# Latent attention and ternary gated MLP on one core: the normed attention input transposed by VectorE blocks and through DRAM instead of on TensorE

## The chip, the cores and the metric

The kernel runs on one core of a Trainium2 chip. The metric is the device time of one execution in microseconds (us); lower is better. Three runs of the kernel before took 1197.63 to 1201.61 us, median 1198.27 us.

## The reference, cut to what matters

```python
x = x + layernorm(attn(layernorm(x)))      # x: 4096 rows (2 x 2048) of 512
x = x + layernorm(ffn(layernorm(x)))
# attn(h), per head of 32 (16 heads, 64 latent keys):
Q = h @ Wq.T + bq;  V = h @ Wv.T + bv
logits = Q . latent / sqrt(32)             # top 4 of 64, softmax over these
out = (weights @ latent + V) @ Wo.T + bo
# ffn(h): weights rounded to -1, 0, 1 times a scale
hidden = silu(h @ Wu.T) * (h @ Wg.T)       # 2048 wide
out = hidden @ Wd.T
```

`h @ Wq.T` on TensorE needs h with its 512 features on the partitions: h^T. How h^T of the attention is made is what the change touches.

## The kernel before, in words

The 4096 rows are worked in eight blocks of 512 rows, each four tiles of 128 rows (t = 0 to 3). All instructions stand in an order written by hand, engine by engine; no scheduler moves them, and each engine works its list in order.

The outer loop (L835) goes over the blocks b; for each it runs the expert layer in 16 chunks e of 128 hidden columns. A chunk is, on TensorE: `up("u", e)` (eight 512-column matmuls into `pu`, L602), `up("g", e)` (eight into `pg`, L602), `down(e-1)` (eight into the four accumulators `acc`, L638). On the other engines: `tanh` of `pu` on ScalarE (L611), `silu` (L614) and `gate` (L619) on VectorE, a cast `hi` on ScalarE (L623), the remainder `lo` on VectorE (L628); `down` needs both `hi` and `lo`. `pu` and `pg` have one buffer each, so `up("u", e+1)` waits for `silu(e)`.

Between these chunk steps, at the places `do(3)`, `do(0)`, `do(1)`, `do(2)`, the program puts in the pieces of the attention of block b + 1. The table is in `pieces` (L764): `put(e, k, f, ...)` puts f at chunk e, place k. The first two blocks' attention is written out apart (`FirstAttention`). For block b + 1 >= 2 (six blocks) the start is:

- at chunk 14 place 2 and chunk 15 place 1 of block b - 1: `a_stats` (mean and variance of each row, VectorE, L234 and L235) and `a_rstd` (POOL, L241 and L242);
- at chunk 0 of block b: `a_apply` (VectorE, L261) writes the normed rows of a tile into a `row` buffer; `a_trans` (L299) makes 4 TensorE transposes of 128 by 128 per tile into PSUM (`pt_a`, L271), 16 per block, and ScalarE copies them into `hT` (L307);
- at chunk 1 place 0: `q(0)` (L310, matmuls at L314), the first reader of `hT`; at places 1 of chunk 1 `l(0)` (logits, L328); further `q`, `l`, `v` (L406) later.

At chunk 0 and 1 the previous block is also finished: `down(15)` runs in chunk 0, then `y_stats` (VectorE), `y_rstd` (POOL), and in chunk 1, behind `gate(1)`, four `y` (VectorE, L261) read the accumulators, which `down(0)` of the new block then overwrites.

One step of the kernel before already transposes by VectorE and DRAM: `z` (L381). VectorE transposes the weights `w` in blocks of 32 by 32 (L383), SP writes the tile `z` to DRAM (`dz`, L388), and four loads of 64 KB each fetch it back with the 32-row groups exchanged (`wT`, L391). All DMAs of the kernel are issued by SP's queue, in program order, and a DMA whose data isn't ready holds up all behind it.

The tiles of x: `load_x(b + 2)` at chunk 4 of block b (chunk 12 for b = 0), into twelve buffers (3 * TT). The same tile feeds the norm, and later the residual sums.

Of the kernel before, what the change touches and what calls it, by code (L numbers as in the profile page):

```python
# [10 lines left out]
F32 = mybir.dt.float32  # L11
F32R = mybir.dt.float32r
BF16 = mybir.dt.bfloat16
AF = mybir.ActivationFunctionType
# [3 lines left out]
P = 128  # L18
# [40 lines left out]
def latent_attention_ternary_glu(  # L59
# [15 lines left out]
    nc = tc.nc  # L75
    NT, D = x_in.shape
    E = wuT.shape[1]
    DC = D // P
    EC = E // P
    TB = 512  # L80
    TT = TB // P
    NB = NT // TB
# [4 lines left out]
    work = ctx.enter_context(tc.tile_pool(name="work", bufs=2))  # L87
    small = ctx.enter_context(tc.tile_pool(name="small", bufs=4))
    dram = ctx.enter_context(tc.tile_pool(name="dram", bufs=3, space=bass.MemoryType.DRAM))
# [7 lines left out]
    def at_psum(name):  # L97
        return ps_at.tile([P, 512], F32, tag="at", name=name)
# [7 lines left out]
    def transposed(which, b, name, dtype):  # L106
        return work.tile([P, DC, TB], dtype, tag=f"{which}{b % 2}", name=name, bufs=1)


    x_tiles = {}  # L110
# [6 lines left out]
    raw = {}  # L117
    late = []
    for q in range(DC):
        w = work.tile([P, D], F32, tag="x", name=f"raw_d_6_{q}", bufs=3 * TT)  # L120
        late.append(w)
    for n, i in RAW_ORDER:
        raw[n, i] = wpool.tile([P, CH], F32, tag="chunk", name=f"raw_{n}_{i}", bufs=6 * DC)
# [4 lines left out]
    def load_x(b):  # L128
        x_tiles[b] = []
        for t in range(TT):  # L130
            xt = work.tile([P, D], F32, tag="x", name=f"x_{b}_{t}", bufs=3 * TT)
            r = b * TB + t * P
            nc.sync.dma_start(out=xt, in_=x_in[r : r + P, :])
            x_tiles[b].append(xt)

    def load_up(n, src):
        for i, (k, h) in enumerate(halves):
            nc.sync.dma_start(
                out=raw[n, i], in_=src[k * P : (k + 1) * P, h * CH : (h + 1) * CH]
            )  # L140
# [5 lines left out]
    bqv_sb = wpool.tile([P, 2, DC], F32, name="bqv_sb")  # L146
# [13 lines left out]
    for i in range(count["d"]):  # L160
        rows = 2 * P if i < 6 else P
        r = i * 2 * P if i < 6 else 12 * P + (i - 6) * P
        nc.sync.dma_start(
            out=raw["d", i].rearrange("p (c n) -> p c n", n=D),
            in_=wdT[r : r + rows, :].rearrange("(c p) n -> p c n", p=P),
# [99 lines left out]
    def row(name):  # L265
        return work.tile([P, D], F32, tag="row", name=name, bufs=4)

    def transpose_row(h, name):
        pt = at_psum(f"pt_{name}")
        for c in range(DC):  # L270
            nc.tensor.transpose(pt[:, c * P : (c + 1) * P], h[:, c * P : (c + 1) * P], ident)  # L271
        return pt.rearrange("p (c k) -> p c k", k=P)
# [3 lines left out]
    class Attention:  # L276
# [9 lines left out]
            self.po = {}  # L286


        def a_stats(self, t):
            self.norm_a.stats(t, x_tiles[self.b][t])  # L290

        def a_rstd(self, lo, hi):
            self.norm_a.rstd(lo, hi)

        def a_apply(self, t):
            self.rows["a", t] = row(f"h_a{self.b}_{t}")
            self.norm_a.apply(self.rows["a", t], x_tiles[self.b][t], t)

        def a_trans(self, t, engine=None):  # L299
            if self.hT is None:  # L300
                self.hT = transposed("X", self.b, f"hT_{self.b}", F32)
            src = transpose_row(self.rows.pop(("a", t)), f"a{self.b}_{t}")
            dst = self.hT[:, :, t * P : (t + 1) * P]
            if engine is nc.vector:
                nc.vector.tensor_copy(dst, src)
            else:
                nc.scalar.copy(dst, src)  # L307


        def q(self, c):  # L310
# [65 lines left out]
            )  # L376

        def z(self, i):  # L381
            z = work.tile([P, 4, P], F32, tag="left", name=f"z_{self.b}_{i}", bufs=2)
            nc.vector.transpose(  # L383
# [11 lines left out]

        def mixed(self, x):
            return x.rearrange("p (t a i) -> p a t i", t=TT, i=32)

# [9 lines left out]

        def y(self, c):
            self.y_pe(c)
            nc.scalar.activation(
                self.mixed(self.attnT[:, c, :]),
                self.pv.pop(c).rearrange("p (a t i) -> p a t i", t=TT, i=32),
                AF.Identity, bias=bqv_sb[:, 1, c : c + 1],
            )

        def y_pe(self, c):
            for pr in range(2):  # L420
# [53 lines left out]


    class FirstAttention(Attention):
        def a_trans_pe(self, t):
            if self.hT is None:
                self.hT = transposed("X", self.b, f"hT_{self.b}", F32)
            self.pt = getattr(self, "pt", {})  # L480
            self.pt[t] = transpose_row(self.rows.pop(("a", t)), f"a{self.b}_{t}")
# [178 lines left out]
    A = FirstAttention(0)  # L660
# [81 lines left out]
    for step in FIRST_STEPS.split():  # L742
        name, numbers = re.fullmatch(r"([a-z]+)([0-9_]*)", step).groups()
# [20 lines left out]
    def pieces(A, after):  # L764

        at = {(e, k): [] for e in range(EC) for k in range(4)}

        def put(e, k, f, *args):
            at[e, k].append(lambda: f(*args))

        if A.b > 1:
            put(0, 0, A.a_apply, 0)
            put(0, 0, A.a_apply, 1)
            put(0, 1, A.a_trans, 0)
            put(0, 1, A.a_trans, 1)
            put(0, 1, A.a_apply, 2)
            put(0, 1, A.a_apply, 3)
            put(0, 2, A.a_trans, 2)
            put(0, 2, A.a_trans, 3)
            put(1, 0, A.q, 0)  # L780
            put(2, 0, A.q, 1)
            put(4, 0, A.q, 2)
            put(6, 0, A.q, 3)
        put(1, 1, A.l, 0)
        put(2, 2, A.l, 1)
        put(5, 1, A.l, 2)
        put(7, 1, A.l, 3)
        for i in range(8):
            put(2 + i, 0, A.m, i)
            put(2 + i, 2, A.r, i)  # L790
            put(3 + i, 3, A.e, i)
            put(3 + i, 1, A.n, i)
            put(3 + i, 1, A.z, i)
        for c in range(DC):
            put(5 + 2 * c, 1, A.v, c)
            put(5 + 2 * c, 1, A.y, c)
        put(11, 2, A.o, 0)
        put(11, 2, A.o, 1)
        put(11, 2, A.o_bias, 0)
        put(12, 0, A.o, 2)  # L800
        put(12, 0, A.o_bias, 1)
        put(12, 0, A.o_rstd, 0, 2)
        put(12, 1, A.o, 3)
        put(12, 1, A.o_bias, 2)
        put(12, 2, A.o_apply, 0)
        put(12, 2, A.o_apply, 1)
        put(12, 2, A.o_bias, 3)
        put(12, 2, A.o_rstd, 2, 4)
        put(13, 0, A.o_apply, 2)
        put(13, 0, A.o_apply, 3)  # L810
        put(13, 1, A.f_stats, 0)
        put(13, 1, A.f_stats, 1)
        put(13, 1, A.f_rstd, 0, 2)
        put(13, 2, A.f_stats, 2)
        put(13, 2, A.f_stats, 3)
        put(13, 2, A.f_rstd, 2, 4)
        put(14, 0, A.f_apply, 0)
        put(14, 0, A.f_apply, 1)
        put(14, 1, A.f_alloc)
        put(14, 1, A.f_trans, 0)  # L820
        put(14, 1, A.f_trans, 1)
        put(14, 1, A.f_apply, 2)
        put(14, 1, A.f_apply, 3)
        put(15, 0, A.f_trans, 2)
        put(15, 0, A.f_trans, 3)
        if after is not None:
            put(14, 2, after.a_stats, 0)
            put(14, 2, after.a_stats, 1)
            put(15, 1, after.a_stats, 2)
            put(15, 1, after.a_stats, 3)  # L830
            put(15, 1, after.a_rstd, 0, 4)
        return at

    prev = None
    for b in range(NB):  # L835
        if b > 0:
            A, nxt = nxt, after
        after = None
        F = Experts(b, (A.hi, A.lo))
        at = {}  # L840
        for e in range(EC):
            if e == (12 if b == 0 else 4) and b + 2 < NB:
                load_x(b + 2)
            if e == 4:
                after = Attention(b + 2) if b + 2 < NB else None
                if b + 1 < NB:
                    later = pieces(nxt, after)
                    at.update({k: v for k, v in later.items() if k[0] >= 4})
            elif e == 0 and b + 1 < NB:
                at.update({k: v for k, v in pieces(nxt, None).items() if k[0] < 4})  # L850

            def do(k):
                for f in at.get((e, k), ()):
                    f()

            def first(place):
                if b == 0:
                    rest(e, place)

            F.up("u", e)  # L860
            do(3)
            F.tanh(e)
            first("tanh")
            do(0)
            F.silu(e)
            F.up("g", e)
            do(1)
            F.gate(e)
            F.high(e)
            first("high")  # L870
            if e > 0:
                F.down(e - 1)
            elif prev is not None:
                prev.down(EC - 1)
            do(2)
            if e == 0 and prev is not None:
                for t in range(TT):
                    prev.y_stats(t)
                prev.y_rstd(0, TT)
            if e == 1 and prev is not None:  # L880
                for t in range(TT):
                    prev.y_out(t)
            F.low(e)
        prev = F
# [52 lines left out]
```

## Time and profile before

| | |
|---|---|
| median of three runs | 1198.27 us |
| the profiled execution | 1200.29 us |
| its span, first to last instruction | 1198.5 us |
| mean granted TensorE clock | 0.994 |
| TensorE (PE) busy | 1165.4 us |
| VectorE (DVE) busy | 823.9 us |
| ScalarE (ACT) busy | 376.7 us |
| GpSimd (POOL) busy | 176.6 us |
| share of the end chain on PE | 91% |

The profile is of one execution. Its chain is followed back from the last instruction: each step to what released it, or to the instruction before it on the same engine. In a timeline a row gives the start, the duration, the engine, the line and the operation; `x8` says that eight instructions were merged into the row. A DVE duration is longer than the distance to the next start, since instructions overlap at their ends; where instructions follow each other at once, the distance is what one costs. SPq rows are the times in which SP issues DMAs, not the transfers.

### The profile page before, as it was taken

To read this page: it belongs to the slowest core of one execution; us is meant where nothing else is said; L and a number is where in the kernel's file an instruction comes from. 1 tells how busy PE (TensorE), PEld (TensorE's weight loads), DVE (VectorE), ACT (ScalarE), POOL (GpSimd) and SP (SyncE) were. 2 spreads that over 40 slices of the span, in tenths; PEclk is the share of its full clock that TensorE was granted. 3 is DMA by queue.
4 is the path that set the end of the run, shared out by engine and by line. 5 is a ranking of instruction groups with operands and counts; after the bars stand their busy time and mean duration, and the time that the engine had idled before them with its cause. 6 is when DMAs were issued, how large, how long until landed. Compare 5 with 4: busy or idle time off the path is not lost.

```text
span 1198.5 us, 14533 instructions
## 1 busy us (share of the span) xinstructions
PE 1165.4 (97%) x4814; PEld 791.9 (66%) x4814; DVE 823.9 (69%) x2887; ACT 376.7 (31%) x667; POOL 176.6 (15%) x215
## 2 busy tenths in 40 slices
PE   8999999999999999999999999999999999999996
PEld 5447665765767666666657666676665866657884
DVE  5876984777757766678757687476884868747344
ACT  4884541332213322133222332123321332212221
POOL 1066001210022000320003200032000320013002
PEclk9899999999999999999999999999999999999998
DMA  9700211021100211002110021100210011100000
GB/s 351 272 0 1 70 63 45 1 97 53 62 1 10 97 53 53 1 36 80 53 45 1 36 88 53 36 1 36 97 58 23 1 50 57 56 16 10 27 1 35
DMA packets 56283, 63.61 MB, mean 53 GB/s; under 512 B 6160, under 2 KB 34832, under 8 KB 56208
## 3 DMA queue, kind: packets, MB, share of 16 engines
q1 hardware_dynamic: 56208, 62.68, 15.1%
q8 instruction: 38, 0.62, 0.2%
q14 instruction: 37, 0.30, 0.1%
HBM read 39.59 MB, written 23.07 MB: 52 GB/s over the span
## 4 chain that ended last, share of the span: by engine, by line
PE 91%; DVE 4%; ACT 2%; DMA 1%; POOL 1%; issue 0%; SPq 0%; POOLq 0%; DVEq 0%; ACTq 0%
PE acc L638 20%; PE pu L602 19%; PE pg L602 19%; PE pv L406 8%; PE po L432 8%; PE pq L314 7%; PE pv L421 3%; PE pl L328 2%; PE pq L490 1%; PE pt_f L271 1%; PE pt_a L271 1%; PE po L558 1%; ACT w L336 1%; DMA raw_u<-in_wuT 1%; DMA lk<-in_latk 1%; DVE left L354 1%
## 5 line engine op out<-in xcount | busy, mean ns | idle before, releaser
L638 PE MATMUL acc<-tern_d,hi 128*128 128x512 f32 x512 | 209.7, 410 | 4.1 <-DVE y L261 4.1
L602 PE MATMUL pg<-hT_f,tern_g 128*128 128x512 f32 x512 | 212.7, 415 | 0.8 <-DVE h L619 0.8
L602 PE MATMUL pu<-hT_f,tern_u 128*128 128x512 f32 x512 | 203.8, 398 | 0.7 <-ACT hT_f L579 0.7
L638 PE MATMUL acc<-tern_d,lo 128*128 128x512 f32 x512 | 200.3, 391 | 0.1
L602 PE MATMUL pu<-lT_f,tern_u 128*128 128x512 f32 x512 | 199.5, 390 | 0.2 <-DVE lT_f L585 0.2
L602 PE MATMUL pg<-lT_f,tern_g 128*128 128x512 f32 x512 | 199.5, 390 | 0.0
L623 ACT CAST hi<-h 128x512 fp32r<-128x512 f32 x128 | 79.2, 618 | 255.0 <-DVE h L619 255.0
L611 ACT ACTIVATE h<-pu,columns 128x512 f32<-128x512 f32 x128 | 87.5, 684 | 223.6 <-PE pu L602 223.1
L614 DVE SCALAR_TENSOR_TENSOR h<-h,pu 128x512 f32<-128x512 f32 x128 | 86.9, 679 | 98.2 <-ACT h L611 98.2
L638 PEld LDWEIGHTS acc<-tern_d,hi 128*128 128x128 f32 x512 | 96.1, 188 | 56.4 <-issue 24.4
L619 DVE TENSOR_TENSOR h<-h,pg 128x512 f32<-128x512 f32 x128 | 85.6, 669 | 63.9 <-PE pg L602 63.0
L628 DVE TENSOR_TENSOR lo<-h,hi 128x512 fp32r<-128x512 f32 x128 | 90.3, 706 | 49.0 <-ACT hi L623 49.0
L602 PEld LDWEIGHTS pg<-hT_f,tern_g 128*128 128x128 f32 x512 | 96.2, 188 | 27.5 <-issue 7.4
L602 PEld LDWEIGHTS pg<-lT_f,tern_g 128*128 128x128 f32 x512 | 96.2, 188 | 26.1 <-issue 7.4
L406 PE MATMUL pv<-hT,wv 128*128 128x512 f32 x224 | 102.1, 598 | 10.1 <-ACT w L336 10.1
L602 PEld LDWEIGHTS pu<-hT_f,tern_u 128*128 128x128 f32 x512 | 96.1, 188 | 23.3 <-issue 1.7
L602 PEld LDWEIGHTS pu<-lT_f,tern_u 128*128 128x128 f32 x512 | 96.2, 188 | 21.6 <-issue 1.7
L638 PEld LDWEIGHTS acc<-tern_d,lo 128*128 128x128 f32 x512 | 96.3, 188 | 20.2 <-issue 1.7
L241 POOL TENSOR_SCALAR rs_o<-mv_o 128x2 f32<-128x2 f32 (+1 forms) x18 | 6.4, 355 | 667.9 <-DVE mv_o L235 667.7
L354 DVE MATCH_REPLACE8 left<-m,w 128x64 f32<-128x64 f32 x512 | 100.2, 210 | 0.0
L432 PE MATMUL po<-wo,attnT 128*128 128x512 f32 x224 | 99.5, 592 | 0.0
L439 DVE TENSOR_TENSOR o<-po,bo_sb 128x512 f32<-128x512 f32 x28 | 19.4, 692 | 100.5 <-PE po L432 100.5
(116 smaller groups left out, 1434.2 us busy)
## 6 DMA issues: line engine op xcount, KB each, us to landing
dz<-z SPq DMA_DIRECT2D x56, 256.0 KB, 2.0
wT<-dz SPq DMA_DIRECT2D x224, 64.0 KB, 1.9
x<-in_x SPq DMA_DIRECT2D x32, 256.0 KB, 3.7
out_x<-x SPq DMA_DIRECT2D x32, 256.0 KB, 2.0
raw_u<-in_wuT SPq DMA_DIRECT2D x8, 512.0 KB, 8.4
raw_g<-in_wgT SPq DMA_DIRECT2D x8, 512.0 KB, 10.2
raw_d<-in_wdT SPq DMA_DIRECT2D x6, 512.0 KB, 11.6
wq<-in_wqT SPq DMA_DIRECT2D x1, 1024.0 KB, 8.0
```

Source lines behind the costliest of these rows:

```text
L314: nc.tensor.matmul(pq, lhsT=wq[:, k, c * P : (c + 1) * P], rhs=self.hT[:, k, :], start=(k == 0), stop=(k == DC - 1),)
L354: nc.vector.match_replace(left[:, g, :], m8[:, g, :], w[:, g, :], TAKEN)
L406: nc.tensor.matmul(self.pv[c], lhsT=wv[:, k, c * P : (c + 1) * P], rhs=self.mixed(self.hT[:, k, :]), start=(k == 0), stop=False,)
L421: nc.tensor.matmul(self.pv[c][pr * HP : (pr + 1) * HP, :], lhsT=lv[:, 2 * c + pr, :], rhs=self.wT.pop(2 * c + pr), start=False, stop=True, ...
L432: nc.tensor.matmul(self.po[t], lhsT=self.attnT[:, c, t * P : (t + 1) * P], rhs=wo[:, c, :], start=(c == 0), stop=(c == DC - 1),)
L602: nc.tensor.matmul(p, lhsT=tern[n, 2 * k + e // 8][:, (e % 8) * P : (e % 8 + 1) * P], rhs=part[:, k, :], start=(k == 0 and i == 0), stop=( ...
L611: nc.scalar.activation(self.h[e], self.pu[e], AF.Tanh, scale=half_u[0])
L614: nc.vector.scalar_tensor_tensor(self.h[e], self.h[e], 1.0, self.pu.pop(e), ALU.add, ALU.mult)
L619: nc.vector.tensor_tensor(self.h[e], self.h[e], self.pg.pop(e), ALU.mult)
L623: nc.scalar.copy(hi, self.h[e])
L628: nc.vector.tensor_tensor(lo, self.h.pop(e), self.hid[e][0].bitcast(F32), ALU.subtract)
L638: nc.tensor.matmul(self.acc[t], lhsT=part[:, t * P : (t + 1) * P], rhs=wd, start=(e == 0 and i == 0), stop=(e == EC - 1 and i == 1),)
```

## The change

For the six blocks b >= 2 the TensorE transposes and ScalarE copies are replaced. The rows of x are loaded a second time into four buffers of their own (`xa`); the norm is applied in place there, one chunk place earlier (chunk 15, place 2, of the block before); VectorE transposes each column group of 128 in blocks of 32 by 32 (`a_blocks`, 16 instructions per block); SP writes four tiles `za` to DRAM (`da`) in runs of 512 bytes and issues sixteen loads of 64 KB, which exchange the 32-row groups (`a_load`). The tokens of `hT` then stand in another order, which the transpose of `z` turns back, so the strided reading in `v` stays and the strided write of `attnT` falls away. The place of `q(0)` is not changed.

```diff
-            xt = work.tile([P, D], F32, tag="x", name=f"x_{b}_{t}", bufs=3 * TT)
+            xt = work.tile([P, D], F32, tag="x", name=f"x_{b}_{t}", bufs=2 * TT)
...
+    def load_normed(b):
+        for t in range(TT):
+            xt = work.tile([P, D], F32, tag="xa", name=f"xa_{b}_{t}", bufs=TT)
+            r = b * TB + t * P
+            nc.sync.dma_start(out=xt, in_=x_in[r : r + P, :])
+            normed[b, t] = xt
...
         def a_apply(self, t):
-            self.rows["a", t] = row(f"h_a{self.b}_{t}")
-            self.norm_a.apply(self.rows["a", t], x_tiles[self.b][t], t)
-        def a_trans(self, t, engine=None):
...
+            self.norm_a.apply(normed[self.b, t], normed[self.b, t], t)
+        def a_blocks(self, c):
+            if c == 0:
+                self.da = dram.tile([P, 4, DC, P], F32, tag="da", name=f"da_{self.b}", bufs=2)
+            z = row(f"za_{self.b}_{c}").rearrange("p (k e) -> p k e", k=4)
+            for t in range(TT):
+                nc.vector.transpose(
+                    z[:, :, 32 * t : 32 * t + 32],
+                    normed[self.b, t][:, c * P : (c + 1) * P].rearrange("p (k j) -> p k j", j=32),
+                )
+            nc.sync.dma_start(out=self.da[:, :, c, :], in_=z)
+        def a_load(self):
+            self.hT = transposed("X", self.b, f"hT_{self.b}", F32)
+            for k in range(4):
+                for c in range(DC):
+                    nc.sync.dma_start(
+                        out=self.hT[32 * k : 32 * k + 32, c, :].rearrange("j (a e) -> j a e", a=4),
+                        in_=self.da.rearrange("(a j) k c e -> k c j a e", j=32)[k, c],
+                    )
...
-            put(0, 0, A.a_apply, 0)
-            put(0, 0, A.a_apply, 1)
-            put(0, 1, A.a_trans, 0)
-            put(0, 1, A.a_trans, 1)
-            put(0, 1, A.a_apply, 2)
-            put(0, 1, A.a_apply, 3)
-            put(0, 2, A.a_trans, 2)
-            put(0, 2, A.a_trans, 3)
+            put(0, 0, A.a_blocks, 0)
+            put(0, 0, A.a_blocks, 1)
+            put(0, 1, A.a_blocks, 2)
+            put(0, 1, A.a_blocks, 3)
+            put(0, 1, A.a_load)
             put(1, 0, A.q, 0)
...
             put(15, 1, after.a_rstd, 0, 4)
+            for t in range(TT):
+                put(15, 2, after.a_apply, t)
...
-            if e == (12 if b == 0 else 4) and b + 2 < NB:
-                load_x(b + 2)
+            if e == 4 and 0 < b < NB - 1:
+                load_x(b + 1)
+            if e == (12 if b == 0 else 6) and b + 2 < NB:
+                load_normed(b + 2)
```

More of the change, by code (lines that the diff above doesn't have):

```diff
@@ L119, in latent_attention_ternary_glu @@
     for q in range(DC):
-        w = work.tile([P, D], F32, tag="x", name=f"raw_d_6_{q}", bufs=3 * TT)
+        w = work.tile([P, D], F32, tag="xa", name=f"raw_d_6_{q}", bufs=TT)
         late.append(w)
@@ L134, in load_x @@
             x_tiles[b].append(xt)
+    normed = {}
+    def load_normed(b):
[4 more added lines that the diff above has]
+            normed[b, t] = xt
     def load_up(n, src):
@@ L289, in a_stats @@
         def a_stats(self, t):
-            self.norm_a.stats(t, x_tiles[self.b][t])
+            self.norm_a.stats(t, normed[self.b, t])
         def a_rstd(self, lo, hi):
@@ L295, in a_apply @@
         def a_apply(self, t):
-            self.rows["a", t] = row(f"h_a{self.b}_{t}")
-            self.norm_a.apply(self.rows["a", t], x_tiles[self.b][t], t)
-        def a_trans(self, t, engine=None):
[L300 to L307, printed above, removed]
+            self.norm_a.apply(normed[self.b, t], normed[self.b, t], t)
[17 more added lines that the diff above has]
+                    )
         def q(self, c):
@@ L394, in z @@
                 )
+        mixes = False
         def mixed(self, x):
@@ L412, in y @@
             self.y_pe(c)
[L413 to L417, printed above, removed]
+            dst, src = self.attnT[:, c, :], self.pv.pop(c)
+            if self.mixes:
+                dst, src = self.mixed(dst), src.rearrange("p (a t i) -> p a t i", t=TT, i=32)
+            nc.scalar.activation(dst, src, AF.Identity, bias=bqv_sb[:, 1, c : c + 1])
         def y_pe(self, c):
@@ L476, in latent_attention_ternary_glu, with a_stats, a_apply @@
     class FirstAttention(Attention):
+        mixes = True
+        def a_stats(self, t):
+            self.norm_a.stats(t, x_tiles[self.b][t])
+        def a_apply(self, t):
+            self.rows["a", t] = row(f"h_a{self.b}_{t}")
+            self.norm_a.apply(self.rows["a", t], x_tiles[self.b][t], t)
         def a_trans_pe(self, t):
```

## The prediction

> **What bounds the kernel now.** I read the busy shares first, then the chain that ended last, then the chain in order of time around one block's start.
>
> ```profile
> PE   1165.4 (97%) x4814; PEld 791.9 (66%) x4814; DVE 823.9 (69%) x2887; ACT 376.7 (31%) x667; POOL 176.6 (15%) x215
> ...
> PE 91%; DVE 4%; ACT 2%; DMA 1%; POOL 1%; issue 0%; SPq 0%; POOLq 0%; DVEq 0%; ACTq 0%
> ```
>
> TensorE is busy 97% of the span, and 91% of the chain is its own queue. So a PE instruction taken out is worth its time, and a wait put in front of a PE instruction costs its whole length. The chain at the start of one of the six blocks (the other five look alike):
>
> ```profile
> 515.18 1.81 PE pu L602 x8
> 516.99 1.82 PE pg L602 x8
> 518.81 0.88 PE pt_a L271 x8
> 519.69 1.85 PE acc L638 x8
> 521.54 0.87 PE pt_a L271 x8
> 522.41 1.83 PE pu L602 x8
> 524.24 3.43 PE pq L314 x8
> 527.68 1.84 PE pg L602 x8
> ```
>
> Chunk 0 begins at 515.18. The sixteen transposes lie directly on the chain, in two groups of eight. The first reader of `hT`, q(0), starts at 524.24 with no gap before it: today everything that makes `hT` is hidden but the 1.75 us of the transposes.
>
> **What the change removes.** Per block 0.88 + 0.87 = 1.75 us of PE, six blocks, 10.5 us. Without it PE would be ready for q(0) at 524.24 - 1.75 = 522.49. The ScalarE copies that go (24 of 590 ns) lie on an engine busy 31%; I cost them at nothing. So do the contiguous write of `attnT`: today's strided one takes 688 ns, the contiguous form of the first block 682.
>
> **What it adds: the new way to hT.** I walk it in this block's times. VectorE and POOL before:
>
> ```profile
> 515.53 0.65 DVE L619 TENSOR_TENSOR h<-h,pg 128x512 f32<-128x512 f32 x1
> 516.88 0.69 DVE L628 TENSOR_TENSOR lo<-h,hi 128x512 fp32r<-128x512 f32 x1 [0.69 <-ACT hi L623]
> 517.48 1.00 DVE L261 TENSOR_SCALAR h_a<-x,mv_a,rs_a 128x512 f32<-128x512 f32 x2
> 518.40 0.68 DVE L614 SCALAR_TENSOR_TENSOR h<-h,pu 128x512 f32<-128x512 f32 x1
> ...
> 515.98 1.01 POOL L242 TENSOR_TENSOR rs_a<-rs_a,minus_half 128x4 f32<-128x4 f32 x1
> ```
>
> 1. The four `a_apply` now stand before lo(15). They need rs_a, ready at 515.98 + 1.01 = 516.99. They start near 517.05 and cost 0.46 each (two from 517.48 to 518.40): 4 x 0.46 = 1.84, until 518.89.
> 2. lo(15) takes 0.60 (516.88 to 517.48), until 519.49. Its reader down(15) reaches PE at 518.81 now, so PE stands some 0.6 us; this disappears in the later wait.
> 3. Eight block transposes (c = 0, 1). The trace has no 128x128 one, only the 128x512 of `z`: 711 ns, next start 0.64 later. On VectorE the 512-element tensor_tensor costs 0.60 start to start, the 32-element one 0.10 (L356, L358), that is 0.50 for 480 elements, about 1.04 ns each; 0.64 - 384 x 0.00104 = 0.24 us. Bounds: a quarter of 0.64, 0.16, and the whole 0.64. I take 0.24, as the 128-element form lies nearest to those short ones. 8 x 0.24 = 1.92, until 521.41. silu(0), queued behind them, is done 0.60 later, at 522.01 instead of 519.0; up("u", 1) waits for it, again inside the later wait.
> 4. Eight more (c = 2, 3): until 523.93, the last one's end near 524.0. gate(0), y_stats and lo(0) follow, some 5 us; all are needed only behind q(0).
> 5. SP issues the last `da` write at about 524.05 and its loads behind it. The nearest rows are `dz` and `wT`:
>
> ```profile
> 549.83 0.33 SPq L388 DMA_DIRECT2D dz<-z  x1
> 551.89 1.75 SPq L391 DMA_DIRECT2D wT<-dz  x4
> ...
> wT<-dz SPq DMA_DIRECT2D x224, 64.0 KB, 1.9
> ```
>
> A 256 KB write is followed by its reader 551.89 - 549.83 = 2.06 us after its issue. `da` has the same bytes in 512-byte runs instead of 2 KB; I add 0.2 (bounds 2.06 and 3.9, the longest landing of these rows). So it has landed at 524.05 + 2.26 = 526.3. The loads are issued at 1.75 / 4 = 0.44 us each and land 1.9 after their issue (1.8 to 3.9). Their order is k outer, c inner: the fourth (k = 0, c = 3) is the first that needs the last write, and in the built program the first matmul of q(0) waits for the four loads of c = 0, the last of which is the thirteenth. That is nine steps after the fourth: 526.3 + 9 x 0.44 = 530.26, landed at **532.2**. The other three matmuls of q(0) wait for loads 14, 15, 16, 0.44 apart, and take 0.86 each, so nothing more is lost.
>
> q(0) starts at 532.2 instead of 524.24: **8.0 us later per block**, the 1.75 us of gain already inside. Nothing gives it back: behind q(0) the chain is the same (pg, then gate(1), the first `y`, down(0)), since gate(1) waits for pg(1).
>
> 6. The clock. PE then stands from about 524 to 532. The trace shows one long stand, at the end; the last matmul starts at 1186.36:
>
> ```profile
> 1188.00:1190.00 2.00, 0.00 (x0) 0.00 (x0) 1.97 (x4) 0.00 (x0) 1.72 (x5) 1.00 0.00 0
> 1190.00:1192.00 2.00, 0.00 (x0) 0.00 (x0) 1.61 (x4) 0.00 (x0) 1.82 (x5) 0.67 0.00 0
> 1192.00:1194.00 2.00, 0.00 (x0) 0.00 (x0) 1.63 (x2) 0.00 (x0) 2.00 (x2) 0.50 0.02 6
> ```
>
> Column 7 (after the five engines' busy times) is the granted clock: full until 4 us after the last matmul, then 0.50. And at the start of the program the warm-up matmuls `ones` take 421 ns in the first five us (first start 1.0) and 275 from about 6.1 on. So an 8 us stand should end at half clock, and q(0) and what follows run so for some 3.4 to 5.1 us; half of it is lost. I take 2.2 us, bounds 0 (rival B) and 2.6.
>
> The Trainium skill ("TensorE: Matmul & The Clock Gate", "What's actually happening") says that the clock falls to half after an idle window of about 3.4 us and is given back after one busy window of that length. By it alone the loss would be half of 3.4, 1.7 us, and the time 3 us less; the start of this trace shows a longer slow stretch.
>
> **The other edits.** The second load of x adds four 256 KB DMAs per block at chunk 6, between the issues of two `z` steps; SP issues them in 1.85 us, in a stretch where it otherwise waits for `z`, and `wT` is needed a chunk later (today PE waits for `wT` 0.8 us in all). Nothing; if that cover went, at most 1.85 us per block. The load of x for the residual is needed at chunk 12. The four `da` writes and sixteen loads stand ahead of the `out_x` stores, which wait for POOL until after q(0) anyway. `a_apply` in place of four `row` buffers frees these for `za`.
>
> **The sum.** 8.0 + 2.2 = 10.2 us per block, times six: 61 us. Against the profiled execution: span 1198.5 + 61 = 1259.5, and 1.8 lie around the span (1200.29 - 1198.5): 1261. The profiled execution lies 2.0 above the median of the runs, so for the median 1198.27 + 61 = **1259 us**.
>
> Both ends: low, transposes at 0.16 (16 x 0.08 = -1.3), the write at 2.06 (-0.2), loads issued at the 0.33 of `dz` (9 x 0.11 = -1.0), clock 1.7 (-0.5): 7.2 per block, 1241. High, write (+1.6) and loads (+2.0) landing at 3.9, clock 2.6 (+0.4): 14.2 per block, 1283.
>
> A rule that speaks against the change: the Trainium skill ("VectorE: DVE Perf Modes", "Rules for kernel authors") gives a 128x128 transpose to TensorE where PSUM is a fit destination, and "The three transpose paths" gives 311 ns to VectorE's and 390 to TensorE's. This trace has TensorE's at 0.87 / 8 = 0.11 us, less than the page; with 311 ns for VectorE's an estimate would be 16 x 0.07 = 1.1 us more per block, 1266.
>
> **Rivals.**
> - A, forecast: `hT` lands after PE is ready, the clock falls: 1259 (1241 to 1283). Chance 0.70.
> - B: the wait is there, but the clock doesn't fall or comes back at once: 6 x 8.0 = 48, 1246. For it: the granted clock reads 1.00 in the slow first five us, so the column doesn't tell all. 0.14.
> - C: a transpose has the cost of the whole 512-element row, 0.64: 16 x 0.40 = 6.4 more per block, 1298; with slow landings 1321. Against it: short VectorE forms cost 0.10 to 0.20. 0.08.
> - D: loads are issued much faster than 0.44 (they have no write between them), and land soon after the last write: q(0) at 526.3 + 1.9 + 1 = 529.2, 5 us and a smaller clock loss of 1 us, 36 in all, 1234. 0.05.
> - E, the other side: the way through DRAM is hidden and the 1.75 us are gained, 1198.27 - 10.5 = 1188. It is one matter, the moment at which the thirteenth load lands: it decides at 522.49 (gain) and 524.24 (no change), and the walk gives 532.2. Even loads of no length would need the last write landed before 524.24, and its transposes end at 524.0. 0.03.
>
> The range 1240 to 1285 holds A, B and most of the low and high ends; C, D and E (0.16) are left out. About 0.3% is what a measurement of this kernel can tell from no change. Faster 0.02, within 0.3% 0.01 (E), slower 0.97.
>
> **What would show it.** In the changed profile, PE pq L336 (or its weight load) must wait for DMA `hT` six times, about 8 us each; pt_a must fall to the 32 of the first two blocks; the mean clock must fall below 0.99, and the first q(0) matmuls after the wait must last nearly twice 592 ns (step 6). If the 128x128 transposes stand far from 0.24 us, step 3 is wrong; if `hT` loads are issued off 0.44 apart or land far from 1.9, step 5 is. No wait at q(0) at all would make the forecast wrong.

## The result and the profile after

| | before | after |
|---|---|---|
| median of 4 runs each, taken together | 1199.79 us | 1264.64 us |
| lowest to highest | 1197.63 to 1201.61 us | 1262.57 to 1267.94 us |
| ratio to before, 95% interval | | 1.0544 [1.0511, 1.0577] |
| profiled execution | 1200.29 us | 1262.57 us |
| its span | 1198.5 us | 1260.8 us |
| mean granted TensorE clock | 0.994 | 0.974 |

The change made the kernel 5.4% slower, 65 us. Two executions in the comparisons below stand far from the others of their kernels, one of "q(0) later" (1251.83 us at a mean clock of 0.933, the others 0.983 to 0.987) and one of the kernel before (5270.72 us), and are left out of the ratios. The lines of the page of after that answer to those shown of before (busy shares; granted clock in forty slices; end chain by engine; the group of q; two of the DMA issues):

```profile
PE 1170.8 (93%) x4718; PEld 785.4 (62%) x4718; DVE 841.3 (67%) x2983; ACT 363.3 (29%) x643; POOL 176.7 (14%) x215
...
PEclk9999999899998999989999899998999989999998
...
PE 80%; DVE 10%; DMA 3%; ACT 2%; SPq 2%; issue 1%; POOL 1%; POOLq 0%; ACTq 0%; DVEq 0%
...
L336 PE MATMUL pq<-hT,wq 128*128 128x512 f32 x192 | 99.8, 668 | 51.8 <-DMA hT<-da 51.8
...
da<-za SPq DMA_DIRECT2D x24, 256.0 KB, 2.7
hT<-da SPq DMA_DIRECT2D x96, 64.0 KB, 2.0
```

TensorE has 96 instructions less and yet 5 us more of busy time, since q's matmuls went from 592 to 668 ns in the mean. Six slices of the clock row, one in each changed block, read 8 (the seventh 8 is the end). TensorE's share of the end chain fell from 91% to 80%, and VectorE, DMAs and SP's queue took it.

The waits of TensorE in after (line, what it waited for: us in all, times, longest), with the rows that before also has left out:

```profile
PE pq L336 <- DMA hT<-da: 51.8, 6, 8.8
...
PE acc L669 <- DVE lo L659: 3.4, 6, 0.6
...
PE pu L633 <- DVE h L645: 1.5, 6, 0.3
```

The new waits ("stands" below: TensorE has work and does none) come six times each: q(0) for the loads of `hT`, down(15) for lo(15), up("u", 1) for silu(0). The other rows that matter are as before (`pv` for `w` 10.1, `acc` for `y` 4.1).

The end chain of after in order of time (start, duration, what), at the block that the prediction walked. Its times stand 20.20 us later here, from the blocks ahead of it:

```profile
536.17 1.02 POOL rs_a L252
537.19 0.03 issue
537.22 1.91 DVE xa L271 x4
539.13 0.60 DVE lo L659
539.73 1.57 DVE za L316 x8
541.30 0.57 DVE h L645
541.87 0.06 DVE za L316
541.93 0.08 issue
542.01 1.43 DVE za L316 x7
543.45 0.02 issue
543.47 2.82 DMA da<-za
546.29 0.02 issue
546.31 0.30 SPq L326
...
550.13 0.44 SPq L326
550.57 0.04 issue
550.62 1.98 DMA hT<-da
552.59 0.14 issue
552.73 5.21 PE pq L336 x8
557.93 1.87 PE pg L633 x8
```

From 537.22 to 552.73 no TensorE row stands on the chain: the norm, the sixteen transposes, the last write, ten loads and a landing carry it (the tenth load's row is that of its transfer, from its issue at 550.62). The last row shows `pg` at full speed again (1.87), so the slow stretch fell on q(0).

**Where the 65 us lie.** I take the start of rs_a of each changed block as a mark. From mark to mark the blocks are 10.7, 11.3, 10.1, 11.0, 9.8 and (to the end) 11.2 us longer than before, 64.1 in all; ahead of the first mark after is 1.8 us earlier, which makes the 62.3 of the spans. Of the 64.1, the three new waits are 51.8 + 3.4 + 1.5 = 56.7, q(0)'s eight matmuls are 14.5 longer (below), and the transposes gone are -10.5: 60.7. The other 3.4, some 0.19 for each of eighteen stands, is probably the overlap of two matmuls: rows of `pu` last 0.39 us but start 0.23 apart, and a wait counted from the end of a row leaves the 0.16 out. This was argued from the rows, not tried.

### The profile page after: what moved, and what is told of

It reads as the page before. It is cut to its first block, busy times and chain, and to the rows that moved or that the text cites. A ratio compares the mean times of both kernels' runs of the same rounds, so it can differ in the third digit from the quotient of the medians.

```text
span 1260.8 us, 14625 instructions
## 1 busy us (share of the span) xinstructions
PE 1170.8 (93%) x4718; PEld 785.4 (62%) x4718; DVE 841.3 (67%) x2983; ACT 363.3 (29%) x643; POOL 176.7 (14%) x215
## 4 chain that ended last, share of the span: by engine, by line
PE 80%; DVE 10%; DMA 3%; ACT 2%; SPq 2%; issue 1%; POOL 1%; POOLq 0%; ACTq 0%; DVEq 0%
PE pg L633 16%; PE acc L669 16%; PE pu L633 16%; PE pv L429 8%; PE pq L336 8%; PE po L454 8%; PE pv L443 2%; PE pq L521 2%; PE pl L350 2%; SPq L326 2%; DVE za L316 1%; DMA da<-za 1%; DVE st_a L244 1%; DVE lT_f L492 1%; DMA hT<-da 1%
## 5 line engine op out<-in xcount | busy, mean ns | idle before, releaser
L336 PE MATMUL pq<-hT,wq 128*128 128x512 f32 x192 | 99.8, 668 | 51.8 <-DMA hT<-da 51.8
L429 PE MATMUL pv<-hT,wv 128*128 128x512 f32 x224 | 102.1, 598 | 10.1 <-ACT w L358 10.1
L336 PEld LDWEIGHTS pq<-hT,wq 128*128 128x128 f32 x192 | 40.9, 217 | 98.0 <-issue 96.5
```

Source lines behind the costliest of these rows:

```text
L336: nc.tensor.matmul(pq, lhsT=wq[:, k, c * P : (c + 1) * P], rhs=self.hT[:, k, :], start=(k == 0), stop=(k == DC - 1),)
L429: nc.tensor.matmul(self.pv[c], lhsT=wv[:, k, c * P : (c + 1) * P], rhs=self.mixed(self.hT[:, k, :]), start=(k == 0), stop=False,)
```

## The experiments

Theory: q(0) stands because the thirteenth load of `hT` lands 8 us late, and the stand lets the clock fall; nothing else in the change costs time. Rivals: the added work itself (VectorE, SP, second load) costs it; the clock doesn't matter; the waits only move. Ratios are to the kernel before on the same chip, whose medians were 1199.4 to 1200.1 us.

### Both ways at once

The loads of `da` go into a tile that nothing reads, and TensorE transposes again, from `xa`.

```diff
-            self.hT = transposed("X", self.b, f"hT_{self.b}", F32)
+            spare = transposed("Y", self.b, f"spare_{self.b}", F32)
...
+        def a_trans(self, t):
+            ...
+            src = transpose_row(normed[self.b, t], f"a{self.b}_{t}")
+            nc.scalar.copy(self.hT[:, :, t * P : (t + 1) * P], src)
...
+            put(0, 1, A.a_trans, 0)
+            put(0, 1, A.a_trans, 1)
...
+            put(0, 2, A.a_trans, 2)
+            put(0, 2, A.a_trans, 3)
```

> Both ways at once: the 16 VectorE block transposes, the da writes and the 16 loads all stay, but they go to a spare tile that nothing reads; hT is made by TensorE transposes of xa as before. Theory W (the loss is TensorE's wait for the loads at q(0), and the half clock behind it): no wait at q(0); what stays is lo(15), made late by the norm ahead of it (0.57 us per block in the changed profile), 6 x 0.6 = 3.4 us: 1203 us, range 1199 to 1208. Rival V (the added work itself, on VectorE and in the DMA queue, is what costs): near the changed kernel's 1264. A time halfway would say that both count.

Measured: 1209.67 us, ratio 1.0083 [1.0062, 1.0103]. All the added work is there, TensorE has its transposes back, and 55 of the 65 us are gone with the dependence on the loads. The result is 1.7 us above the range. The expected wait for lo(15) isn't among TensorE's waits; this one is, and it makes up 7.7 of the 9.7 us over before:

```profile
PE pq L342 <- ACT hT L335: 7.7, 6, 1.3
```

The block transposes make gate(0) late, the cast hi(0) stands behind it in ScalarE's list, and the copies of the last two `hT` tiles behind that (timeline: hi(0) 524.70, copies 525.23). So the added VectorE work isn't free where it stands: a price of up to 1.3 us per block shows once the great wait is gone.

### The second load of x alone

x is loaded twice and normed in place, at the old places; TensorE transposes.

```diff
-            put(0, 0, A.a_blocks, 0)
...
+            put(0, 0, A.a_apply, 0)
+            put(0, 0, A.a_apply, 1)
+            put(0, 1, A.a_trans, 0)
...
-            for t in range(TT):
-                put(15, 2, after.a_apply, t)
```

> One part of the change alone: x is loaded a second time into xa and normed there in place; the norm stands at its old place in chunk 0 and the transposes are TensorE's. Theory W: SP has room at chunk 6, so 1200 us, within 3 us of the kernel before. Rival (the second load delays the z loads or the residual's x): at most 1.85 us of issue per block, six blocks, up to 1211.

Measured: 1200.21 us, ratio 1.0008 [0.9997, 1.0019]. The second load costs nothing that can be seen.

### TensorE kept busy while it waits

Ten matmuls into a PSUM tile that nothing reads stand ahead of q(0).

```diff
+        def fill(self):
+            pf = at_psum(f"fill_{self.b}")
+            for i in range(10):
+                nc.tensor.matmul(pf, lhsT=ident, rhs=wq[:, 0, :], start=True, stop=True)
...
+            put(1, 0, A.fill)
             put(1, 0, A.q, 0)
```

> The changed kernel with ten matmuls of 512 columns in float32 (0.86 us each by the q rows, 8.6 us in all) put on TensorE ahead of q(0), into a PSUM tile that nothing reads: they fill the wait of 8.5 to 8.8 us, so that TensorE never stands. Theory W says that the wait has a second price, the clock: the first q(0) took 5.1 to 6.6 us instead of 3.43, 14.5 us over the six blocks. With the filler q(0) should take 3.43 and the time be 1264 - 14.5 = 1250, range 1246 to 1254. Rival (q(0) is slow for another reason, such as loads still landing): q(0) stays at 5 to 6 us and the time at 1262 to 1267.

Measured: 1252.05 us, ratio 1.0440 [1.0420, 1.0461]; 12.6 us less than after, mean clock 0.995. The group of q:

```profile
L341 PE MATMUL pq<-hT,wq 128*128 128x512 f32 x192 | 86.7, 594 | 1.4 <-DMA hT<-da 1.3
```

q's matmuls are back at 594 ns, with the loads as late as in after. The clock is a price of its own, about 2.1 us per block, and the rival without it falls. It may be a little more: in four of the six blocks q(0) has no wait left for the loads, so there the fillers lasted at least as long as the wait.

### q(0) later

q(0) goes two places back, and the steps that hang on it with it.

```diff
-            put(1, 0, A.q, 0)
+            put(1, 2, A.q, 0)
+            put(2, 0, A.l, 0)
...
-        put(1, 1, A.l, 0)
+        if A.b < 2:
+            put(1, 1, A.l, 0)
...
-            put(2 + i, 0, A.m, i)
+            put(2 + i, 2 if A.b > 1 and i == 0 else 0, A.m, i)
```

> The changed kernel with q(0) two steps later on TensorE (behind down(0) of chunk 1 instead of behind up u of chunk 1), l(0) into chunk 2 place 0 and m(0) to chunk 2 place 2; nothing on SP or ahead of it on VectorE moves. Theory W: up g, the gate and y, and down(0), some 6.2 us of the changed chain, then stand before the loads have landed; a wait of about 2.6 us stays, too short for the clock to fall. Per block 8.0 us less than the changed kernel, 6 x 8.0 = 48: 1216 us, range 1208 to 1224. Rival V (added work is the cost): still 1255 to 1264.

Measured: 1232.55, 1232.66 and 1236.37 us, ratio 1.0284 [1.0265, 1.0303], above the range. The waits are read from a further execution of the same kernel:

> The kernel with q(0) two steps later once more, for a second profile: that run's time was 1234.5 against 1216 expected, and its profile has a clock of 0.933 throughout. Expected here: TensorE's wait is at down(0), for y, some 4 us per block, as the transposes put y_stats and so rs_y and y later; about 1233 us.

Measured: 1233.65 us, span 1231.9. Its waits of TensorE:

```profile
PE acc L669 <- DVE y L271: 27.1, 7, 4.2
...
PE pq L336 <- ACT w L358: 4.1, 6, 0.7
PE acc L669 <- DVE lo L659: 3.5, 6, 0.6
```

No wait for a DMA is left, but down(0) now waits for the four `y` (before: 4.1 in all). The `y` stand in VectorE's list behind the sixteen transposes, y_stats and rs_y. Timeline of VectorE in the same kernel, the chain that makes them late:

```profile
531.11 1.66 DVE L316 STREAM_TRANSPOSE za<-xa 128x128 f32<-128x128 f32 x8
532.68 0.65 DVE L645 SCALAR_TENSOR_TENSOR h<-h,pu 128x512 f32<-128x512 f32 x1
533.26 1.65 DVE L316 STREAM_TRANSPOSE za<-xa 128x128 f32<-128x128 f32 x8
...
540.91 2.97 DVE L271 TENSOR_SCALAR y<-acc,mv_y,rs_y 128x512 f32<-128x512 f32 x4 [0.25 <-POOL rs_y L254]
```

The stand ahead of down(0) is 4.2 us long, and the clock falls behind it after all. The end chain of the same kernel has down(0) as

```profile
541.86 3.55 PE acc L669 x8
```

where the eight of down(15) took 1.85 in before. From the trace's clock, TensorE works some 22 us at half clock behind the six stands, about 11 us lost (an estimate). With the new waits (23.0 for `y`, 4.1 for `w` ahead of q(0), 3.5 for lo(15), 1.6 for silu(0)) and the transposes gone (-10.5) that makes 32.7 of the 33.4 us by which this span is longer.

So half of the price goes by moving the reader, and the other half comes back as a new wait and a fall of the clock behind it: the transposes stand in the busiest part of VectorE's list, where the old block is finished.

### The order of the loads, and two queues

First c outer, k inner, so that the first matmul needs the first four loads and not the thirteenth; then, in a kernel by itself, the old order with the loads of k = 2, 3 issued by ScalarE.

```diff
-            for k in range(4):
-                for c in range(DC):
+            for c in range(DC):
+                for k in range(4):
```

> The changed kernel with the sixteen loads in the other order, c outer and k inner, so that the four loads of c = 0, which the first matmul of q(0) needs, depend on the first da write alone and are issued first; the number of loads and the work are the same. Theory W (the thirteenth load in the queue sets the end of the wait): loads of c = 0 issued from about 0.1 us behind the last da issue, landed some 4 us after TensorE is ready instead of 8.7; then each next matmul comes as its four loads land, 1.9 us apart; q(0) ends about 3.3 us earlier than in the changed kernel, or 2.4 where the clock still falls. 6 x 3 = 18: 1246 us, range 1242 to 1254. Rival (all loads land together, the write's landing is what counts): no gain, 1262 to 1267.

```diff
-                    nc.sync.dma_start(
+                    (nc.sync if k < 2 else nc.scalar).dma_start(
```

> The changed kernel with the loads of k = 2, 3 issued by ScalarE's queue and those of k = 0, 1 by SP's. Theory W with the issue of 0.47 us per load as the largest part of the path: the last load that the first matmul needs is the second behind the last write instead of the tenth; q(0) starts some 3.8 us earlier, 6 x 3.8 = 23: 1242 us, range 1236 to 1256 since ScalarE stands in its queue for the write meanwhile and hi(0) and tanh(1) come late. Rival (the transfers, not their issue, are slow): 1258 or more.

Measured: 1244.57 us, ratio 1.0375 [1.0358, 1.0393], and 1249.60 us, ratio 1.0413 [1.0397, 1.0428]. The waits at q(0), c outer first, two queues second:

```profile
PE pq L336 <- DMA hT<-da: 26.8, 12, 4.4
```

```profile
PE pq L336 <- DMA hT<-da: 35.5, 6, 6.2
```

With c outer the wait falls from 51.8 to 26.8, 4.2 us per block, near the nine steps of 0.48 that the first matmul no longer waits for: the loads' issue is half of the wait. (Its four loads no longer wait for the last write's landing either; in after that held up the fourth load's issue by half a us, 0.92 behind the third instead of 0.47.) With two queues it falls by 2.7 only, not by the 3.8 expected. The tile view of `hT` in that kernel, for ScalarE's loads of one block, says part of the reason (issue to landing: least, median, most):

```profile
DMA to landing us min/median/max: 2.3/2.5/3.0
```

A load lands 2.5 us after its issue instead of 2.0, and the write of `da` 2.9 instead of 2.7: 0.7 of the 1.1 us that are missing. Besides, hi(0) stands behind ScalarE's eight loads, 11.35 us after its last work. In both kernels the clock keeps its price (busy time of `pq` 101.3 and 102.7; after 99.8, before 86.2).

### The whole way earlier

Statistics at chunk 11, norm at 12, transposes at 13 and 14 (one chunk later for the first changed block), loads at chunk 15.

```diff
-            z = row(f"za_{self.b}_{c}").rearrange("p (k e) -> p k e", k=4)
+            z = work.tile([P, 4, P], F32, tag="w", name=f"za_{self.b}_{c}", bufs=4)
...
+            put(11 + d, 0, after.a_stats, 0)
...
+            put(12 + d, 1, after.a_apply, 0)
...
+            put(13 + d, 0, after.a_blocks, 0)
+            put(13 + d, 0, after.a_blocks, 1)
+            put(13 + d, 2, after.a_blocks, 2)
+            put(14, 2, after.a_blocks, 3)
+            put(15, 2, after.a_load)
```

> All of the new way moved earlier, where VectorE has idle time: for five of the six blocks the statistics of xa at chunk 11, the norm at chunk 12, the transposes at chunks 13 and 14, into the four buffers of w, free there; the first of the six one chunk later, since its xa comes at chunk 11; the sixteen loads behind chunk 15 place 2, where the buffer of hT comes free. The first load can be issued when up g of chunk 15 is done, some 9 us before q(0); the thirteenth lands 0.1 + 12 x 0.47 + 2.0 = 7.7 us later. Theory W: no wait at q(0), full clock, and the 1.75 us of TensorE transposes are gained per block: 1200 - 10.5 = 1189 us, range 1186 to 1195. Rival V (VectorE's added work costs wherever it stands): 1205 or more. Rival (loads that wait in SP's queue hold up others): out_x is behind them only; no loss expected.

Measured: 1200.80 us, ratio 1.0007 [0.9998, 1.0017], above the range. The wait at q(0) and the clock's price are gone, but not a us is gained on before. TensorE's waits and VectorE's timeline:

```profile
PE pt_f L281 <- DVE h_f L271: 7.5, 6, 1.3
```

```profile
499.16 1.66 DVE L316 STREAM_TRANSPOSE za<-xa 128x128 f32<-128x128 f32 x8
...
505.11 0.86 DVE L316 STREAM_TRANSPOSE za<-xa 128x128 f32<-128x128 f32 x4
505.89 0.65 DVE L659 TENSOR_TENSOR lo<-h,hi 128x512 fp32r<-128x512 f32 x1
506.46 0.99 DVE L271 TENSOR_SCALAR h_f<-x,mv_f,rs_f 128x512 f32<-128x512 f32 x2
```

Twelve transposes, 2.4 us, stand ahead of `h_f`, which TensorE transposes next. Of the 1.75 us gained, 1.3 became this wait. From mark to mark (rs_y here) the blocks are 145.0 us long against 144.9 of before, so another half a us per block went that the waits don't show; it isn't explained. In the same kernel VectorE stood idle for 7.08 us in chunk 11, until 480.64.

### The way into VectorE's idle stretch

For the last five blocks statistics, norm and transposes go to chunks 10 and 11, ahead of the first `o_bias`; then the same with one step of the first changed block put back.

```diff
+        if after is not None and after.b > 2:
+            put(10, 2, after.a_stats, 0)
...
+            put(11, 0, after.a_rstd, 0, 4)
+            for t in range(TT):
+                put(11, 2, after.a_apply, t)
+            for c in range(DC):
+                put(11, 2, after.a_blocks, c)
         put(11, 2, A.o, 0)
...
+            if after.b == 2:
+                put(14, 0, after.a_blocks, 0)
+                put(14, 0, after.a_blocks, 1)
+                put(14, 2, after.a_blocks, 2)
+                put(15, 2, after.a_blocks, 3)
```

> For the last five of the six blocks the statistics, the norm and all sixteen block transposes are moved into the stretch of chunk 11 in which VectorE stood idle for 7.1 us in the early version (473.5 to 480.6); they need 4 x 0.46 + 16 x 0.196 = 5.0 us, and rs_a some 2 us behind the statistics. The sixth (the first that is changed) keeps the early version's places, since its second load of x comes too late for chunk 11. Theory (the way through DRAM is free where its sixteen loads land ahead of q(0) and where no other VectorE work is pushed behind the transposes): no wait at q(0) and none at pt_f for these five blocks, TensorE keeps 1.75 us in each, 8.75 in all, and the block that keeps its place gives 0 to 1.75: 1200 - 9 = 1191, range 1187 to 1196. Rival (VectorE's added 5 us per block cost TensorE about as much wherever they stand, by a wait elsewhere): 1198 or more.

Measured: 1195.78 us, ratio 0.9968 [0.9955, 0.9980]. From mark to mark (rs_y) four blocks are 143.06 to 143.09 us long instead of 144.9; the first changed one is 147.98, with the only wait for the loads that is left (3.07 us), since its last four transposes had slipped to chunk 15. The result lies in the range, but 5 us from the 1191 expected.

```diff
-                put(15, 2, after.a_blocks, 3)
+                put(14, 2, after.a_blocks, 3)
```

> As the run before it (1195.78 us), but the last four block transposes of the first changed block stand at chunk 14, place 2, as in the early version, instead of chunk 15, place 2, where they made its loads land late: q(0) of that block waited 3.07 us and the block became 147.98 us long instead of 144.86, while the other five went from 144.9 to 143.1. Theory (only that late load stood against the gain): the block becomes about 145 long, 3.0 less, so 1192.8; counted from the kernel before, 1199.9 - 5 x 1.8 = 1191. Range 1189 to 1194, no wait for a DMA at q(0). Rival (the wait isn't from those four transposes): 1195 or more.

Measured: **1190.93 us**, ratio 0.9931 [0.9916, 0.9945]: 0.7% less than before, and 74 us less than after. The first changed block is 142.97 us long, 5.0 less and not 3.0: its wait of 3.07 had also let the clock fall, for 3.41 us. VectorE's timeline in chunk 11 and the group of q on its page:

```profile
469.12 0.69 DVE L650 TENSOR_TENSOR h<-h,pg 128x512 f32<-128x512 f32 x1
469.87 1.92 DVE L271 TENSOR_SCALAR xa<-xa,mv_a,rs_a 128x512 f32<-128x512 f32 x4
471.70 3.20 DVE L316 STREAM_TRANSPOSE za<-xa 128x128 f32<-128x128 f32 x16
477.40 0.69 DVE L461 TENSOR_TENSOR o<-po,bo_sb 128x512 f32<-128x512 f32 x1 [2.50 <-PE po L454]
```

```profile
L336 PE MATMUL pq<-hT,wq 128*128 128x512 f32 x192 | 86.3, 592 | 0.0
```

Norm and transposes, 5.0 us of VectorE, lie in a stretch in which it had nothing to do, and 2.5 us are left of that. The same DMAs that cost 65 us in after now end ahead of their reader: the loads, which stand behind chunk 15, are issued from 509.30 on, the thirteenth lands at 517.07, and q(0) starts at 518.36. The 1.75 us of transposes that the change took from TensorE are a gain of 1.8 per block.

## Why the prediction was right

Forecast 1259 (1240 to 1285), measured 1264.64. Step by step, with the times of after less 20.20:

| step | predicted | measured |
|---|---|---|
| 1. norm starts, ends | 517.05, 518.89 | 517.02, 518.93 |
| 2. TensorE stands for lo(15) | 0.6 | 0.56 (3.4 in 6) |
| 3, 4. one block transpose | 0.24 | 0.196 (1.57 / 8) |
| last transpose done | 524.0 | 523.25 |
| 5. last write lands after | 2.26 | 2.82 |
| write landed | 526.3 | 526.09 |
| loads apart | 0.44 | 0.48 (546.31 to 550.62 is nine steps) |
| thirteenth load issued | 530.26 | 530.42 |
| a load lands after | 1.9 | 2.0 |
| q(0) starts | 532.2 | 532.53 |
| later than before | 8.0 | 8.3 |
| 6. clock, per block | 2.2 | 2.4 (12.6 / 6 = 2.1 by the fillers) |

The mechanism, its place and its six occurrences were right. In step 3 the term was 20% too dear (0.7 us for sixteen), in step 5 the write was 0.56 too cheap: it took 0.76 us more than the write of `dz` with its 2 KB runs, not the 0.2 that I added. The two nearly cancel, which is luck. So, in part, is step 6: its 2.2 was taken from the slow stretch at the start of the program, while the price moves between 1.7 and 3.1 with the place of the stand (last section). The sum was 61 us and 64.9 were measured: q(0) came 0.3 us later than forecast and the clock cost 0.2 more, six times each, 3 of the 3.9 us. The block walked confirms it by itself: 8.3 + 1.8 (its own clock loss) = 10.1, and it is 10.1 longer. The rest of the distance to 1259 is that before itself had 1199.79 in this comparison, not 1198.27.

"The other edits: nothing" holds for the second load of x (1200.21). It doesn't hold for VectorE's added work where it stands: both ways at once cost 9.7 us, 7.7 of them by a copy behind hi(0). In the prediction's own kernel this is hidden in the greater wait. That gate(0), y_stats and lo(0) are "needed only behind q(0)" was true with q(0) where it is, but only there: with q(0) moved, down(0) waits for `y`, (27.1 - 4.1) / 6 = 3.8 us more per block.

The rivals: B, no fall of the clock, is refuted by the fillers; C by the 0.196; D by the 0.48 between loads; E by the wait, though E is what the last kernel does, once the transposes end 43 us ahead of q(0) (474.90 and 518.36) and the thirteenth load lands 1.3 us ahead of it.

The rule of the Trainium skill that gives a 128x128 transpose to TensorE where PSUM is a fit destination ("VectorE: DVE Perf Modes", "Rules for kernel authors") agrees with after (1264.64 us) and not with the last kernel (1190.93). The 311 and 390 ns that the prediction quotes beside it are for bf16; the tiles here are float32. What decided was not the price of a transpose (0.196 us here against 0.11 on TensorE) but which engine had the time, and whether the way back through DRAM ended ahead of its reader.

## What to carry to other kernels

A step that goes from the bounding engine to another one and through DRAM has a length of its own (here 4 x 0.46 + 16 x 0.20 + 2.8 + 9 x 0.48 + 2.0, with lo(15) and silu(0) between: 15.5 us from the norm to q(0)); it pays only if it starts that much ahead of its reader, so move the producer as far as its data allows before judging it. Put added work into a stretch in which its engine's timeline shows idle time, not merely on an engine with a low share: the same sixteen transposes made TensorE wait 3.8 us per block for `y`, 1.3 for `h_f`, and not at all in chunk 11. Where several loads feed one reader, issue first those that its first instruction needs.

## What the runs showed of the hardware

**The clock moves on a grid.** The granted clock of after in slices of 1 us around one q(0) (busy time of PE, PEld, DVE, ACT, POOL; then clock, DMA share, GB/s):

```profile
548.00:549.00 1.00, 0.00 (x0) 0.00 (x0) 0.40 (x1) 0.00 (x0) 0.98 (x1) 1.00 0.49 140
549.00:550.00 1.00, 0.00 (x0) 0.00 (x0) 0.00 (x0) 0.00 (x0) 0.30 (x2) 0.50 0.51 147
...
555.00:556.00 1.00, 1.00 (x2) 0.34 (x1) 0.00 (x0) 0.00 (x0) 0.00 (x0) 0.59 0.00 0
556.00:557.00 1.00, 1.00 (x4) 0.47 (x3) 0.00 (x0) 0.00 (x0) 0.00 (x0) 1.00 0.00 0
```

It falls at 549.0, 5 us after the end of the last matmul (544.03), and is back at 555.82 (0.59 in a slice is 82% at half clock). From slices of half a us, the six stands of after:

| clock falls | q(0) starts | clock back | half of q(0)'s slow stretch | q(0) longer than 3.43 by |
|---|---|---|---|---|
| 234.97 | 241.02 | 245.21 | 2.10 | 2.32 |
| 391.98 | 396.41 | 402.22 | 2.90 | 3.13 |
| 549.00 | 552.73 | 555.82 | 1.55 | 1.78 |
| 702.60 | 707.55 | 712.84 | 2.65 | 2.87 |
| 859.61 | 863.48 | 866.44 | 1.48 | 1.71 |
| 1013.21 | 1018.50 | 1023.45 | 2.48 | 2.70 |

The slow stretches are 6.82 or 10.24 us long, two or three times 3.41, and all the times of the run lie on one grid of 3.41. So a stand costs half of the time from TensorE's return to the end of the first grid step that it keeps busy, here 1.5 to 2.9 us (2.96 us of work in a step were enough, 2.40 were not); the last column's further 0.22 isn't explained by the clock. The upper bound of 2.6 in step 6 was too low for three of the six. It also shows why less waiting didn't lessen this price: with c outer, stands of 3.8 to 4.4 us had slow stretches of 3.41 or 6.83. The stands of 1.3 us in the early version cost no clock.

But the length of a stand doesn't settle it. Ahead of the last block's down(0) TensorE stands 1.67 us for `y` in before and in the last kernel alike (before: 1103.86 to 1105.53; last kernel: 1092.60 to 1094.27). In before the clock stays at full speed. The last kernel's, in the same slices of 1 us:

```profile
1095.00:1096.00 1.00, 1.00 (x4) 0.49 (x4) 1.00 (x2) 0.00 (x0) 1.00 (x2) 1.00 0.07 16
1096.00:1097.00 1.00, 1.00 (x4) 0.57 (x3) 1.00 (x2) 0.00 (x0) 1.00 (x2) 0.50 0.63 236
```

It falls at 1096.00 for 3.41 us, and from the last rs_y to the end the kernel is 1.4 us longer than before. The grid step from 1092.59 to 1096.00 holds that stand whole; in before a grid point, counted back from the fall at 1190.69, lies at 1105.36 and cuts it. So what a stand costs depends on where it lies on the grid, and a change of some us far ahead can move it; by the luck of this place, the last kernel's profiled execution gains 1.4 us less than its blocks give.

The Trainium skill ("TensorE: Matmul & The Clock Gate", "What's actually happening") says just this of the window: it runs freely, and lasts 3413 ns. The prediction had used only its length, as if a window began with TensorE's return; the runs agree with the page on this when its free running is taken in. That the clock fell behind a stand of 1.67 us shows that a window need not be idle from end to end.

**DMA prices in these runs.** A 256 KB write to DRAM in runs of 512 bytes (`da`) takes SP 0.51 us to issue and lands in 2.7 (the first of the four of a block in 2.6, the last in 2.8), against 0.33 and 2.0 in runs of 2 KB (`dz`). Sixteen loads of 64 KB on one queue take 8.2 to 8.4 us to issue in after, where they wait for the writes, and 7.7 to 7.9 with c outer; split on two queues, each lands half a us later (2.5 and 2.6 against 2.0).
